# Transformer block on one core: shared keys for shared buffers in a build-time planner, and an earlier transpose of the first token block

## The chip, the cores and the metric

The kernel runs on one core of a Trainium2 chip. The metric is the device time of one execution in microseconds (us). All engines of the core work from their own instruction queues in order and wait for each other through semaphores: TensorE (PE in the profile; PEld is its weight load), VectorE (DVE), ScalarE (ACT), GpSimd (POOL) and SyncE (SP), which issues nearly all DMAs here.

## The reference

Input x is 8 x 1024 x 512 in float32, the condition 8 x 512. Hidden width is 2048, and there are 16 heads of 32.

```python
mod = silu(condition) @ Wada + bada
sh_a, sc_a, gt_a, sh_m, sc_m, gt_m = split(mod, 6, axis=1)
xm = layernorm(x, g1, be1) * (1 + sc_a) + sh_a
x = x + gt_a * (causal_attention(xm @ Wqkv) @ Wproj + bproj)
xm = layernorm(x, g2, be2) * (1 + sc_m) + sh_m
return x + gt_m * (gelu(xm @ W1 + b1) @ W2 + b2)
```

## The kernel before

**Tiling.** The tokens are cut into 16 blocks of 512 (two halves, h = 0 and 1, of each of 8 batch rows). A block passes through: normalisation into tiles `hat` (`normalize`), transposition and modulation into `xm` (`modulated`; its sums `t` for the fast products), K, Q and V, attention, the output projection (`project_out`), and the MLP (`up`, `down`). The weight products use Strassen's scheme (`strassen`, `down`): seven half-size products in place of eight, with sums of weight pieces and of activations, and partial results in tiles `p1`, `u2`, `u4`.

**Attention.** A head group is four heads. For each group, `scores` computes Q·K with one mask and one maximum over each strip (lines 1175, 1187, 1195); `split_maxima` splits the maxima into three bf16 parts `mcols` (lines 1216 to 1219), on GpSimd or VectorE; `maxima_rows` turns them into a row by matmul (line 1235). `weights_T` computes K·Q with the row subtracted (lines 1261 and 1272) and the exponential on ScalarE into one of three slots `pT` (line 1284), and GpSimd masks the diagonal (line 1289). `weigh` multiplies by V into `po` (line 1312). In `attend`, GpSimd adds each later strip into the first strip's `pT` (line 1396), in place: it may do so only when `weigh` has read that first strip. `finish` sums over partitions by matmul (line 1330); ScalarE copies that to `rec` and `po` to `top` (lines 1336 and 1339), VectorE inverts `rec` in four parts (line 1345), and GpSimd multiplies them into Q's place (line 1350). `rec`, `top`, `p1`, `u2` and `u4` have one buffer each, the tag `y` has two.

**PSUM.** The scores' tile `st` takes four banks, `po` one. The three others, `banks`, serve every linear product, the transposes, line 1235 and line 1330. `lin_bank` takes the one that is free soonest.

**Order.** The order of every engine's instructions is fixed while the program is built. A planner keeps a modelled clock for each engine (`now`) and two tables: `written[key]`, when a value is there, and `left[key]`, when its last reader is done.

```python
def due(reads=(), writes=()):
    t = 0.0
    for k in reads:
        t = max(t, written.get(k, 0.0))
    for k in writes:
        t = max(t, left.get(k, 0.0))
    return t
```

`sooner` and `either` pick the engine of a copy or sum from these, `split_maxima` picks its own, and `step_aside` decides before each attention step whether to issue linear work (the next matmuls of `plan`, four at a time) first. The linear work is a generator `linear` over `plan`, with side threads for transposes and the last products of a Strassen step; each yields what it will read and write, and `work` advances the one whose wait ends first. The hardware's own waits are by semaphores on the real buffers, so a wrong key makes the plan wrong but not the result. Where a key has the step's name in it (`("rec", n, g)`), the buffer's earlier user has another key, and the planner does not see that the write must wait for that user.

**Opening.** SyncE loads the condition, the first block, the eight pieces of Wada for `("mod", 0)` and `("mod", 1)`, and the pieces of K's weights. `modulation(i)` is 128 small matmuls (line 199 with 8 columns). `norm_columns` makes the gain and the shift on VectorE from both. Then `("at", 0)` starts the transposes of the first block (line 594) with their modulation on ScalarE or VectorE (lines 604 and 598), and `("k", 0)` issues its four weight sums on VectorE (line 649) and the first products (line 199).

Of the kernel before, what the change touches and what calls it, by code (L numbers as in the profile page):

```python
# [22 lines left out]
def kernel(  # L23
# [201 lines left out]
    def mlp_steps(n):  # L225
        return [("u", n, i) for i in range(NQ)] + [("d", n, part) for part in range(4)]

    plan = {
        -1: [("mod", 0), ("mod", 1), ("norm_columns_a",), ("at", 0), ("load_xa", 1)]
        + [("k", 0), ("norm_a", 1), ("q", 0), ("at", 1), ("v", 0)],  # L230
        0: [("load_xa", 2), ("preps",), ("k", 1), ("norm_a", 2), ("gates", "a"), ("q", 1)]
        + [("mod", 3), ("at", 2), ("v", 1), ("mod", 4), ("k", 2), ("gates", "m"), ("columns_m",)],
# [175 lines left out]
    def modulation(i):  # L408
        at = take(4)
        part = {kf: halves(j) for kf, j in zip(RAW, at)}  # L410
        yield [], [BANK]
        bank = lin_bank()
        pm = banks[bank][:, : NC * B].rearrange("p (c b) -> p c b", b=B)
        for c in range(NC):
            for k in range(NC):
                w = part[k // 2, c // 2][:, k % 2, ts(c % 2, P)]
                matmul(pm[:, c, :], w, condT[:, k, :], k == 0, k == NC - 1, bank=bank)
                note("PE", 90)
                yield [], []
        release(*at)  # L420
        combine_out(
            modT[:, ts(i, NC), :],
            bank,
            pm,
            cols[:, O_BADA + i * NC : O_BADA + (i + 1) * NC].unsqueeze(2).to_broadcast([P, NC, B]),
        )
# [16 lines left out]
        return gain, shift  # L443

    columns_of = {}
    gate_rows = {}

    kept_rows = {}
# [115 lines left out]
        for t in range(NTT):  # L564
            add_job(lambda t=t: statistics(t), [sources[t]], key[0] == "m")

    def modulated(key, gain, shift, b, guards):
        for t in ("B11", "B21", "B22", "T1", "T2", "T3", "T4"):
            written[key, t] = NEVER
        yield [("hat", key, 0), *guards], [BANK]  # L570
        got = hats.pop(key)
        xm = act.tile([P, NC, TB], F32, tag="xm", name=f"xm_{key}")
        sums = act.tile([P, 3, 2, HB], F32, tag="t", name=f"t_{key}")
        one, two = slice(0, 2), slice(2, 4)
        left_half, right_half = slice(0, HB), slice(HB, TB)
        part = {
            "B11": xm[:, one, left_half],
            "B21": xm[:, two, left_half],
            "B22": xm[:, two, right_half],
            "T1": xm[:, one, right_half],  # L580
            "T2": sums[:, 0, :, :],
            "T3": sums[:, 1, :, :],
            "T4": sums[:, 2, :, :],
        }
        xm_of[key] = part
        at = {t: (key, t) for t in part}
        for c in range(NC):
            if c:
                yield [("hat", key, 0)], [BANK]
            bank = lin_bank()  # L590
            for t in range(NTT):
                if t:
                    yield [("hat", key, t)], []
                nc.tensor.transpose(banks[bank][:, ts(t, P)], got[t][:, ts(c, P)], ident)  # L594
                note_pe(TR, "whole", [("hat", key, t)], [("l", bank)])
            writes = [at["B11"], at["T1"]] if c < 2 else [at["B21"], at["B22"]]
            if sooner([("l", bank)], writes, 770, 780) == "DVE":
                nc.vector.tensor_scalar(
                    xm[:, c, :], banks[bank], gain[:, c, b : b + 1], shift[:, c, b : b + 1],
                    ALU.mult, ALU.add,  # L600
                )
                note("DVE", 770, [("l", bank)], writes)
            else:
                nc.scalar.activation(
                    xm[:, c, :], banks[bank], AF.Identity,
                    bias=shift[:, c, b : b + 1], scale=gain[:, c, b : b + 1],
                )
                note_act(780, None, [("l", bank)], writes)
            live[bank] = False
            if c == 1:  # L610
                nc.vector.tensor_tensor(part["T1"], part["T1"], part["B11"], ALU.subtract)
                note("DVE", 700, [at["B11"], at["T1"]], [at["T1"]], port=True)
        nc.vector.tensor_tensor(part["T2"], part["B22"], part["T1"], ALU.subtract)  # L613
        note("DVE", 700, [at["B22"], at["T1"]], [at["T2"]], port=True)
        for out, a, b in (("T3", "T2", "B11"), ("T4", "B21", "T2")):
            either(part[out], part[a], part[b], ALU.subtract, [at[a], at[b]], [at[out]])
# [74 lines left out]
    def strassen(step, x, dest, target, row, done):  # L691
# [43 lines left out]
        def partial(kind):  # L735
            return tmp.tile([P, 2, HB], F32, tag=kind, name=f"{kind}_{name}", bufs=1)

        k1, k2, k4 = (("part", name, i) for i in (1, 2, 4))
        a = yield from product("A11", "B11")
        p1 = partial("p1")  # L740
        copy_out(p1, a, blocks_of(a), [k1], last=False)
# [66 lines left out]
        )  # L808

    residual, stored = {}, {}  # L810
    LANDING = 10000

    def add_to(xt, other, reads, writes, op=ALU.add):
# [2 lines left out]
    def project_out(n):  # L816
        at = take(NC)
        yield [("attended", n)], []
        attT = qTs.pop(n)
        tiles = [residual[n][:, t, :] for t in range(NTT)]  # L820
        for t, xt in enumerate(tiles):
            xt_job = lambda t=t, xt=xt: add_to(xt, gate_rows["gba"], [("row", "gba")], [("xr", n, t)])
            pool_jobs.append((xt_job, [("xr", n, t)]))
        for t, xt in enumerate(tiles):
            bank = yield from accumulate(
                [(attT[:, c, ts(t, P)], piece(at[c])) for c in range(NC)], [("att", n)]
            )
            tag, bufs = ("hat", NTT) if n == NB - 1 else ("y", 2)
            y = tmp.tile([P, D], F32, tag=tag, name=f"y_{n}_{t}", bufs=bufs)
            ky = ("y", n, t)  # L830
            combine_out(y, bank, banks[bank], gate_rows["ga"], [("row", "ga")], [ky], ALU.mult)
            add_to(xt, y, [ky], [("xr", n, t)])
        release(*at)
        run_pool_jobs(True)
        normalize(tiles, f"m{n}", [("xr", n, t) for t in range(NTT)])
# [50 lines left out]
    def down(n, part):  # L886
# [42 lines left out]
            return tmp.tile([P, 2, HB], F32, tag=tag, name=f"{kind}_d_{n}", bufs=bufs)  # L929

        def key(kind):
            return ("down", n, kind)

        got = partials
        if part == 0:
# [10 lines left out]
        elif part == 1:  # L946
            bank, ps = yield from product("B22")
            got["v3"] = stage("v3", "y", 2)
            combine_out(got["v3"], bank, ps, got["u5"], [key("u5")], [key("v3")])
            combine(nc.vector, "B22", "B22", "B12")  # L950
            combine(nc.gpsimd, "B11", "B22", "B11")
            bank, ps = yield from product("B21")
            y = stage("y11", "y", 2)
            combine_out(y, bank, ps, got["u1"], [key("u1")], [key("y11")])
            combine(nc.gpsimd, "B21", "B21", "B22")
            settle(n, 0, 0, y, key("y11"))
# [7 lines left out]
        else:  # L964
# [6 lines left out]
            store(n, 1)  # L971
            bank, ps = yield from product("B21")
            y = stage("y21", "y", 2)
            combine_out(y, bank, ps, u3, [key("u3")], [key("y21")])
            settle(n, 1, 0, y, key("y21"))
            store(n, 0)
# [4 lines left out]
    def perform(step):  # L981
# [2 lines left out]
            yield from modulation(step[1])  # L984
        elif kind == "norm_columns_a":
            columns_of["a"] = norm_columns("a", 0, 1, O_G1, O_BE1)
        elif kind == "gates":
            yield from gates(step[1])
        elif kind == "columns_m":
# [20 lines left out]
        elif kind == "at":  # L1010
            n = step[1]
            guards = [("m used", n - 3)] if n > 2 else [("v done", 0)] if n == 2 else []
            start(modulated(f"a{n}", *columns_of["a"], blocks[n][0], guards))
        elif kind == "mt":
            n = step[1]
            guards = [("v done", n + 1)]
            start(modulated(f"m{n}", *columns_of["m"], blocks[n][0], guards))
        elif kind == "k":
            yield [("free for k", step[1])], []
            yield from project_T(step, kTs, kvp, "kT", lambda: None)  # L1020
# [33 lines left out]
    def start(it):  # L1054
        thread = [it, None]
        sides.append(thread)
        advance(thread)
# [264 lines left out]
    def finish(n, g):  # L1322
# [9 lines left out]
        free_p.append(slot)  # L1332
        top = tmp.tile([P, TB], F32, tag="top", name=f"top_{n}_{g}", bufs=1)
        rec = tmp.tile([P, TB], F32, tag="rec", name=f"rec_{n}_{g}", bufs=1)
        kr = ("rec", n, g)
        nc.scalar.copy(rec, banks[bank])  # L1336
        note_act(585, None, [("l", bank)], [kr])
        live[bank] = False
        nc.scalar.copy(top, outs.pop((n, g)))
        note_act(585, None, ["po"], [("top", n, g)])  # L1340
        part = TB // 4

        def invert(i):
# [4 lines left out]
        def quotient():  # L1348
            invert(3)
            nc.gpsimd.tensor_tensor(qTs[n][:, g, :], top, rec, ALU.mult)  # L1350
            note("POOL", 1285, [kr, ("top", n, g)], [("att", n)])
            if g == NC - 1:
                written["attended", n] = 0.0

# [4 lines left out]
    def attend():  # L1359
        previous = None  # L1360
        for n in range(NB):
# [19 lines left out]
            for g, k, upto in slots:  # L1381
# [9 lines left out]
                if k > 0:  # L1391
                    acc, first = totals[n, g]
                    for _, c0, w in parts:
                        for j in range(HPG):
                            into = acc[:, j, TB - w :]
                            nc.gpsimd.tensor_tensor(into, into, pT[:, j, c0 : c0 + w], ALU.add)  # L1396
                            note("POOL", 230 + 2.07 * w, [("p", slot), ("p", first)], [("acc", n, g)])
                previous = (n, g, parts, pT, slot, k == n_slots - 1)
                while unit_at[0] < upto:
                    ns = score_need(*units[unit_at[0]])  # L1400
# [109 lines left out]
```

## Time and profile before

| | us |
|---|---|
| median of 3 runs | 3730.38 |
| lowest to highest | 3725.5 to 3731.06 |
| profiled execution, own time | 3731.66 |
| its span in the trace | 3729.9 |
| TensorE busy in it | 3598.8 |
| VectorE busy | 2135.3 |
| GpSimd busy | 2034.5 |
| ScalarE busy | 1341.6 |

The mean granted TensorE clock of the profiled execution is 0.988. The trace repeats itself with every second token block, that is with every batch row, about every 452 us: the same instructions stand at 913.47, 1365.55 and 1817.72 us.

A timeline row has the start and the length in us, the engine, the line, the operation, the tile written and those read, shapes, the count of merged instructions, and in brackets the idle time of the engine before it with what ended it. A row of waits has the waiting instruction, what it waited for, the total in us, the number of times and the longest.

### The profile page before, as it was taken

What the parts mean: (1) busy time and instruction counts of PE and PEld (TensorE: products, weight loads), DVE (VectorE), ACT (ScalarE), POOL (GpSimd) and SP (SyncE); (2) the same over time, 40 slices, a digit from 0 to 9 for tenths busy, and PEclk for the clock granted to TensorE, in tenths of its full rate; (3) what the DMA queues carried; (4) which work ended last, traced back from release to release, by engine and by line L of the source; (5) the groups of instructions that cost most, each with busy time, mean ns of one, the idle gap of its engine ahead of it and who ended that gap; (6) DMA issues with size and microseconds to landing.
All of it is one profiled execution on the core that took longest, in us unless ns stands there. A gap on an engine that the chain in (4) does not pass through costs nothing.

```text
span 3729.9 us, 121143 instructions
## 1 busy us (share of the span) xinstructions
PE 3598.8 (96%) x54821; PEld 1769.8 (47%) x54821; DVE 2135.3 (57%) x2402; ACT 1341.6 (36%) x1436; POOL 2034.5 (55%) x2080
## 2 busy tenths in 40 slices
PE   8889999999999999999999999999999999998999
PEld 4424445444454444544445454444544445454445
DVE  5756665564745547465565665646556464654542
ACT  2334334252333524335152451524425243341421
POOL 1576645655455663566536664456654556444661
PEclk9989999999999999999999999999999999999999
DMA  6633333433334333433334333343333433234334
GB/s 200 196 117 99 116 92 105 127 104 117 106 110 119 105 121 106 138 97 98 120 106 135 97 98 117 106 133 103 101 112 106 135 103 118 91 106 123 90 108 132
DMA packets 307893, 430.34 MB, mean 115 GB/s; under 512 B 25900, under 2 KB 176236, under 8 KB 307380
## 3 DMA queue, kind: packets, MB, share of 16 engines
q1 hardware_dynamic: 307264, 422.56, 37.2%
q8 instruction: 432, 7.08, 0.8%
q14 instruction: 81, 0.66, 0.1%
q10 hardware_dynamic: 116, 0.03, 0.0%
HBM read 394.12 MB, written 28.38 MB: 113 GB/s over the span
## 4 chain that ended last, share of the span: by engine, by line
PE 85%; DVE 7%; POOL 3%; ACT 3%; issue 2%; DMA 0%; SPq 0%; ACTq 0%; POOLq 0%; DVEq 0%
PE bank L199 57%; PE st L1261 8%; PE sc L1175 8%; PE po L1312 7%; POOL pT L1396 2%; DVE mx L1195 2%; PE st L1272 2%; PE bank L594 2%; PE bank L1330 1%; DVE hT L901 1%; ACT pT L1284 1%; DVE xr L156 1%; ACT L546 1%; DVE sc L1187 1%; DVE rec L1345 1%
## 5 line engine op out<-in xcount | busy, mean ns | idle before, releaser
L1396 POOL TENSOR_TENSOR pT<-pT,pT 128x512 f32<-128x512 f32 (+3 forms) x1280 | 1201.9, 973 | 557.0 <-ACT pT L1284 386.0
L1284 ACT ACTIVATE pT<-st 128x2048 f32<-128x2048 f32 (+1 forms) x320 | 546.3, 1707 | 1061.9 <-PE st L1272 1007.4
L199 PE MATMUL bank<-w,hT 128*32 128x256 f32 x14336 | 810.0, 380 | 5.0 <-DVE hT L901 2.1
L1195 DVE TENSOR_REDUCE mx<-sc 128x4 f32<-128x2048 f32 (+3 forms) x384 | 668.9, 1756 | 216.2 <-PE sc L1175 209.0
L199 PEld LDWEIGHTS bank<-w,hT 128*32 128x32 f32 x14336 | 454.0, 110 | 358.4 <-issue 61.7
L199 PE MATMUL bank<-xm_m,w 128*32 128x256 f32 x8192 | 503.8, 380 | 0.5 <-DVE u_u L191 0.5
L1289 POOL TENSOR_SCALAR_AFFINE_SELECT pT<-pT 128x512 f32<-128x512 f32 x256 | 176.1, 700 | 553.1 <-ACT pT L1284 552.7
L199 PE MATMUL bank<-t_m,w 128*32 128x256 f32 x6144 | 384.4, 380 | 2.4 <-DVE t_m L613 1.0
L1261 PE MATMUL st<-qT,kT 32*128 32x512 f32 (+3 forms) x3072 | 343.1, 531 | 27.3 <-DVE mx L1195 27.2
L199 PEld LDWEIGHTS bank<-xm_m,w 128*32 128x32 f32 x8192 | 255.0, 110 | 238.7 <-issue 77.8
L1175 PE MATMUL sc<-kT,qT 32*128 32x512 f32 (+3 forms) x3072 | 344.7, 533 | 11.2 <-DVE mx L1195 6.6
L1187 DVE TENSOR_TENSOR sc<-sc,mask 128x512 f32<-128x512 f32 (+1 forms) x192 | 167.9, 875 | 320.6 <-PE sc L1175 286.5
L1312 PE MATMUL po<-pT,v 128*32 128x512 f32 (+3 forms) x3072 | 319.0, 503 | 4.5 <-POOL pT L1289 4.4
L199 PEld LDWEIGHTS bank<-t_m,w 128*32 128x32 f32 x6144 | 192.0, 110 | 179.6 <-issue 52.0
L199 PE MATMUL bank<-xm_a,w 128*32 128x256 f32 x3968 | 245.6, 383 | 10.0 <-ACT qT L186 4.9
L199 PE MATMUL bank<-w,qT 128*32 128x512 f32 x2048 | 249.3, 614 | 6.1 <-POOL qT L1350 3.2
L1345 DVE RECIPROCAL rec<-rec 128x128 f32<-128x128 f32 x256 | 224.0, 917 | 20.1 <-ACT rec L1336 20.1
L1261 PEld LDWEIGHTS st<-qT,kT 32*128 32x128 f32 x3072 | 128.1, 185 | 195.2 <-issue 67.8
L1175 PEld LDWEIGHTS sc<-kT,qT 32*128 32x128 f32 x3072 | 128.3, 186 | 185.6 <-ACT pT L1284 87.8
L191 DVE TENSOR_TENSOR hT<-bank,u_u 128x512 f32<-128x512 f32 x192 | 130.6, 686 | 122.4 <-PE bank L199 119.8
L199 PE MATMUL bank<-t_a,w 128*32 128x256 f32 x2944 | 186.4, 382 | 13.1 <-ACT rec L1336 13.1
L199 PEld LDWEIGHTS bank<-xm_a,w 128*32 128x32 f32 x3968 | 122.5, 110 | 120.5 <-issue 31.5
(181 smaller groups left out, 3536.9 us busy)
## 6 DMA issues: line engine op xcount, KB each, us to landing
w<-in_L_cond_W_dram SPq DMA_DIRECT2D x384, 256.0 KB, 2.9
w<-kept_up_S SPq DMA_DIRECT2D x256, 256.0 KB, 2.7
w<-kept_down_S SPq DMA_DIRECT2D x256, 256.0 KB, 2.6
w<-kept_qkv_S SPq DMA_DIRECT2D x180, 256.0 KB, 3.0
w<-in_L_cond_Wqkv_dram SPq DMA_DIRECT2D x147, 256.0 KB, 3.4
hat<-in_x_dram SPq DMA_DIRECT2D x64, 256.0 KB, 3.3
w<-in_L_cond_Wproj_dram SPq DMA_DIRECT2D x64, 256.0 KB, 3.2
xr<-in_x_dram SPq DMA_DIRECT2D x64, 256.0 KB, 4.6
```

The source lines that it names most:

```text
L191: nc.vector.tensor_tensor(out, src, other, op)
L199: nc.tensor.matmul(ps[r, :], lhsT[:, r], rhs, start=start, stop=stop, skip_group_check=True)
L594: nc.tensor.transpose(banks[bank][:, ts(t, P)], got[t][:, ts(c, P)], ident)
L1175: nc.tensor.matmul(sc[:, j, c0 : c0 + w], qTs[n][r, g, ts(qt, P)], keys_of(n, kh)[r, g, :w], start=True, stop=True, skip_group_check=True,)
L1187: nc.vector.tensor_tensor(diagonal, diagonal, mask[:, :span].unsqueeze(1).to_broadcast([P, HPG, span]), ALU.add,)
L1195: nc.vector.tensor_reduce(mx[:, kh, qt, :], sc[:, :, c0 : c0 + w], axis=AX.X, op=ALU.max)
L1261: nc.tensor.matmul(st[:, j, c0 : c0 + w], kT[r, g, ts(k % NTT, P)], qT[r, g, TB - w :], start=(c0 == 0), stop=False, skip_group_check=True,)
L1284: nc.scalar.activation(pT[:, :, :used], st[:, :, :used], AF.Exp, scale=scale)
L1289: nc.gpsimd.affine_select(diagonal, diagonal, pattern=[[0, HPG], [1, P]], compare_op=ALU.is_ge, fill=0.0, base=0, channel_multiplier=-1,)
L1312: nc.tensor.matmul(po[r, TB - w :], v[:, k % NTT, g * P + j * hd : g * P + (j + 1) * hd], pT[:, j, c0 : c0 + w], start=(k == 0), stop=last ...
L1345: nc.vector.reciprocal(some, some)
L1396: nc.gpsimd.tensor_tensor(into, into, pT[:, j, c0 : c0 + w], ALU.add)
```

## The change

It has two parts. In the first, keys of the planner's tables are named after the buffer instead of the step: `rec`, `top`, `p1`, `u2`, `u4`, and the two buffers of `y` in turn; and the accumulation of line 1396 counts the first strip's slot as written instead of read, so that the planner makes it wait for `weigh`. In the second, the first block's 16 transposes go into the scores' four banks and are issued between `("mod", 0)` and `("mod", 1)`, whose matmuls wait for the key `early` that is set when the transposes are issued; the modulation of its four chunks is issued after `norm_columns`. No arithmetic is added or taken away.

```diff
     plan = {
-        -1: [("mod", 0), ("mod", 1), ("norm_columns_a",), ("at", 0), ("load_xa", 1)]
+        -1: [("at", 0), ("mod", 0), ("mod", 1), ("norm_columns_a",), ("load_xa", 1)]
...
     def modulation(i):
...
-        yield [], [BANK]
+        yield ["early"] if i == 1 else [], [BANK]
...
+    written["columns"] = written["early"] = NEVER
...
-    def modulated(key, gain, shift, b, guards):
+    def modulated(key, b, guards):
...
+        def modulate(c, place, source):
+            gain, shift = columns_of[key[0]]
             writes = [at["B11"], at["T1"]] if c < 2 else [at["B21"], at["B22"]]
-            if sooner([("l", bank)], writes, 770, 780) == "DVE":
+            if sooner([source], writes, 770, 780) == "DVE":
...
+        if key == "a0":
+
+            early = ps_st.tile([P, NC, TB], F32, tag="st", name="early")
+        for c in range(NC):
+            if key != "a0":
+                if c:
+                    yield [("hat", key, 0)], [BANK]
+                bank = lin_bank()
+                place, source = banks[bank], ("l", bank)
+            else:
+                place, source = early[:, c, :], "st"
+            for t in range(NTT):
+                if t or c:
+                    yield [("hat", key, t)], []
+                nc.tensor.transpose(place[:, ts(t, P)], got[t][:, ts(c, P)], ident)
+                note_pe(TR, "whole", [("hat", key, t)], [source])
+            if key != "a0":
+                modulate(c, place, source)
+                live[bank] = False
+        if key == "a0":
+            written["early"] = 0.0
+            yield ["columns"], []
+            for c in range(NC):
+                modulate(c, early[:, c, :], "st")
...
-        k1, k2, k4 = (("part", name, i) for i in (1, 2, 4))
+        k1, k2, k4 = "p1", "u2", "u4"
...
+    y_count, y_keys = [0], {}
+
+    def y_key(kind, new=False):
+
+        if kind not in y_keys or new:
+            y_keys[kind] = ("y", y_count[0] % 2)
+            y_count[0] += 1
+        return y_keys[kind]
...
-            ky = ("y", n, t)
+            ky = ("y", n, t) if n == NB - 1 else y_key("proj", True)
...
         def key(kind):
-            return ("down", n, kind)
+            return {"u1": "p1", "u3": "p1", "u5": "u4", "u2": "u2"}.get(kind) or y_key(kind)
...
         elif kind == "norm_columns_a":
             columns_of["a"] = norm_columns("a", 0, 1, O_G1, O_BE1)
+            written["columns"] = 0.0
...
-        kr = ("rec", n, g)
+        kr = "rec"
...
-        note_act(585, None, ["po"], [("top", n, g)])
+        note_act(585, None, ["po"], ["top"])
...
-                            note("POOL", 230 + 2.07 * w, [("p", slot), ("p", first)], [("acc", n, g)])
+                            note("POOL", 230 + 2.07 * w, [("p", slot)], [("acc", n, g), ("p", first)])
```

More of the change, by code (lines that the diff above doesn't have):

```diff
@@ L586, in modulated @@
         at = {t: (key, t) for t in part}
[L587 to L595, printed above, removed]
+        def modulate(c, place, source):
+            gain, shift = columns_of[key[0]]
             writes = [at["B11"], at["T1"]] if c < 2 else [at["B21"], at["B22"]]
-            if sooner([("l", bank)], writes, 770, 780) == "DVE":
+            if sooner([source], writes, 770, 780) == "DVE":
                 nc.vector.tensor_scalar(
-                    xm[:, c, :], banks[bank], gain[:, c, b : b + 1], shift[:, c, b : b + 1],
+                    xm[:, c, :], place, gain[:, c, b : b + 1], shift[:, c, b : b + 1],
                     ALU.mult, ALU.add,
                 )
-                note("DVE", 770, [("l", bank)], writes)
+                note("DVE", 770, [source], writes)
             else:
                 nc.scalar.activation(
-                    xm[:, c, :], banks[bank], AF.Identity,
+                    xm[:, c, :], place, AF.Identity,
                     bias=shift[:, c, b : b + 1], scale=gain[:, c, b : b + 1],
                 )
-                note_act(780, None, [("l", bank)], writes)
-            live[bank] = False
+                note_act(780, None, [source], writes)
             if c == 1:
@@ L948, in down @@
             got["v3"] = stage("v3", "y", 2)
+            y_key("v3", True)
             combine_out(got["v3"], bank, ps, got["u5"], [key("u5")], [key("v3")])
@@ L953, in down @@
             y = stage("y11", "y", 2)
+            y_key("y11", True)
             combine_out(y, bank, ps, got["u1"], [key("u1")], [key("y11")])
@@ L973, in down @@
             y = stage("y21", "y", 2)
+            y_key("y21", True)
             combine_out(y, bank, ps, u3, [key("u3")], [key("y21")])
@@ L1012, in perform @@
             guards = [("m used", n - 3)] if n > 2 else [("v done", 0)] if n == 2 else []
-            start(modulated(f"a{n}", *columns_of["a"], blocks[n][0], guards))
+            start(modulated(f"a{n}", blocks[n][0], guards))
         elif kind == "mt":
@@ L1016, in perform @@
             guards = [("v done", n + 1)]
-            start(modulated(f"m{n}", *columns_of["m"], blocks[n][0], guards))
+            start(modulated(f"m{n}", blocks[n][0], guards))
         elif kind == "k":
@@ L1350, in quotient @@
             nc.gpsimd.tensor_tensor(qTs[n][:, g, :], top, rec, ALU.mult)
-            note("POOL", 1285, [kr, ("top", n, g)], [("att", n)])
+            note("POOL", 1285, [kr, "top"], [("att", n)])
             if g == NC - 1:
```

## The prediction

> **What bounds the kernel now.** I read the page first. TensorE is busy nearly all the time and its clock is full outside the opening and the end, so only its idle time and its slow stretches can be won back: 3729.9 - 3598.8 = 131 us, plus what a halved clock costs.
>
> ```profile
> PE 3598.8 (96%) x54821; PEld 1769.8 (47%) x54821; DVE 2135.3 (57%) x2402; ACT 1341.6 (36%) x1436; POOL 2034.5 (55%) x2080
> PEclk9989999999999999999999999999999999999999
> ```
>
> Next I read TensorE's own waits. The list is short, and two rows of it bear on keys that the change renames; the waits of the other engines show the buffer behind each.
>
> ```profile
> PE bank L1235 <- POOL mcols L1219: 19.8, 8, 2.8
> PE bank L199 <- ACT rec L1336: 13.6, 8, 1.9
> ...
> POOL pT L1396 <- PE po L1312: 163.4, 13, 20.9
> ...
> ACT rec L1336 <- POOL qT L1350: 37.3, 7, 5.3
> ```
>
> GpSimd's accumulation waits for the reader of its in-place target (L1312), and ScalarE's copy into the one buffer `rec` waits for the quotient that still reads it (L1350). Neither wait is in the planner's tables now. The timeline shows what they do to TensorE, once in every pair of blocks.
>
> ```profile
> 913.47 5.52 POOL L1396 TENSOR_TENSOR pT<-pT,pT 128x384 f32<-128x384 f32 x8 [11.25 <-PE po L1312]
> 918.93 0.25 POOL L1216 CAST mcols<-mx 128x16 bf16<-128x16 f32 x1
> 920.21 0.41 PE L1235 MATMUL bank<-ident_b,mcols 128*32 128x128 bf16 x16 [2.70 <-POOL mcols L1219]
> ...
> 961.65 1.26 POOL L1350 TENSOR_TENSOR qT<-top,rec 128x512 f32<-128x512 f32 x1 [3.33 <-DVE rec L1345]
> 962.94 0.58 ACT L1336 COPY rec<-bank 128x512 f32<-128x512 f32 x1 [5.33 <-POOL qT L1350]
> 963.58 1.93 PE L199 MATMUL bank<-t_a,w 128*32 128x256 f32 x32 [1.87 <-ACT rec L1336]
> ```
>
> Stall one: the maxima are ready at 916.07 (L1195, 914.85 + 1.22), but the split was given to GpSimd, which is in the accumulation until 919.0; TensorE stands still for 2.70 us. Stall two: a bank is held until `rec` may be written; TensorE stands still for 1.87 us, then 0.62 and 0.70 us more behind copies (p_q at 965.52, then qT) that stand behind `rec` on ScalarE.
>
> **Part by part: the accumulation's target counted.** Stall one comes seven times: 2.76 + 2.70 + 5 x 2.69 = 18.9 us. The clock follows it. The windows after six of the seven show the granted clock at half, the fourth does not:
>
> ```profile
> 921.50:924.80 3.30, 3.30 (x16) 0.52 (x8) 0.00 (x0) 0.00 (x0) 3.22 (x5) 0.50 0.00 0
> 1825.00:1828.40 3.40, 3.40 (x40) 1.06 (x36) 0.62 (x1) 0.50 (x1) 3.32 (x6) 1.00 0.00 0
> ```
>
> The Trainium skill (TensorE: Matmul & The Clock Gate, section "What's actually happening") has the clock halved only after an idle window of about 3.4 us; by it a gap of 2.7 us costs no clock, and the sum for this stall would be 18.9 us. The trace differs, so I price it from the trace: from the end of stall one to the end of stall two are the same instructions in every pair, and they take
>
> ```profile
> 1824.46 0.35 PE L1235 MATMUL bank<-ident_b,mcols 128*32 128x128 bf16 x12 [2.69 <-POOL mcols L1219]
> 1866.19 0.64 PE L199 MATMUL bank<-t_a,w 128*32 128x256 f32 x8 [1.88 <-ACT rec L1336]
> 2278.78 0.41 PE L1235 MATMUL bank<-ident_b,mcols 128*32 128x128 bf16 x16 [2.69 <-POOL mcols L1219]
> 2322.16 0.62 PE L199 MATMUL bank<-t_a,w 128*32 128x256 f32 x5 [1.88 <-ACT rec L1336]
> ```
>
> 41.73 us without a halved window, 43.38 with one, and in the last pair 44.59 with two (3185.28 to 3229.87): 1.65 for one, 2.86 for two. Five single ones and a double make 5 x 1.65 + 2.86 = 11.1 us. Together stall one is worth 30.0 us. That is the measured upper end; its lower end is that only the engine changes. The change lets the planner see GpSimd busy until 919, so it gives the split to VectorE. There, beside a running accumulation, the nearest row (944.05 to 946.79, another split beside L1396) takes 0.20 + 0.51 + 0.96 + 0.96 = 2.63 us against four pitches of 0.33 on GpSimd. Starting behind the y combine at 916.73 it ends at 919.4, and L1235 starts some 0.7 us earlier than 920.21: 7 x 0.7 = 5 us. But the planner will also see, for the first time, that the split takes until then, and `step_aside` then issues linear matmuls in the gap. They are there: the projection's matmuls (w,qT) go on right behind the stall, in an accumulation that already has its bank. At the nearest row, 944.92, 64 such matmuls stood in the gap and L1235 waited for nothing. I take 26 of the 30, leaving half a microsecond at each place for a fill that comes in whole groups of four.
>
> **rec and top counted.** Stall two is 1.88 + 0.62 + 0.70 = 3.2 us, seven times: 22.4 us at most. The planner will now know that the bank is held, but I see nothing it could run instead. The tile `st` waits for the maxima that VectorE ends at 965.07, the K tail's banks wait for combines behind VectorE's four reciprocals (958.21, 3.35 us), and `rec` cannot be written before 962.9 whatever is planned. What it can do is put p_q and qT on VectorE, off the queue behind `rec`, `top` and the table load; VectorE is free for them at 965.07, against 965.52 on ScalarE. I take 0.6 us each, 4 us. Bounds: 22.4 us gained; 5 us lost (0.7 each) if the copies then queue behind a reduction.
>
> **p1, u2, u4, y counted.** No row of TensorE's waits names such a reuse with more than a single case (y, 2.8 us at 3395.65, in the last block, whose keys stay). I take nothing; bounds 5 us either way. A change of order at these places is covered by the linear work that keeps TensorE at 98% to 100% between the stalls.
>
> **The opening.** The transposes leave the place behind the second modulation and stand in front of it:
>
> ```profile
> 13.00 2.93 ACT L557 ACTIVATE hat<-hat,offset_a,rstd_a 128x512 f32<-128x512 f32 x4 [0.44 <-DVE offset_a L549]
> 17.56 0.72 PE L199 MATMUL bank<-condT,w 128*32 128x8 f32 x40 [2.74 <-issue]
> 18.21 3.68 PE L594 MATMUL bank<-ident,hat 128*128 128x128 f32 x16
> 19.40 0.78 ACT L604 ACTIVATE xm_a<-bank,shifta,gaina 128x512 f32<-128x512 f32 x1 [3.47 <-PE bank L594]
> 22.62 3.64 PE L199 MATMUL bank<-xm_a,w 128*32 128x256 f32 x32 [0.73 <-DVE xm_a L598]
> ```
>
> They need the fourth `hat`, at 15.93. Thirteen remain then, at a pitch of 0.226 us ((3.68 - 0.29) / 15) and a tail of 0.29: 19.1. Behind them in TensorE's queue stand all 128 matmuls of the second modulation, 2.25 us by their rows (64 in 1.17 to 1.22, so 0.016 us each, plus a tail): 21.35. VectorE takes the modulation off at 18.35 now, and gain and shift are there 1.05 us later, at 19.40: so 22.4. The last chunk that the first product waits for is now on VectorE, behind the four weight sums (21.76, 0.80 us). After the change the chunks go one after another on ScalarE, since VectorE is in those sums: the second ends at 24.05, and the first product starts at 24.1 instead of 22.62. Loss 1.5 us. The gain side: the idle 2.74 us ahead of 17.56, which no semaphore ends, would lie under the wait for `hat`; if the clock, full from about 27.1, keeps its place in time, half the loss comes back. The loss side: if that idle time belongs to the instructions and comes again behind the transposes, 1.5 + 2.7 = 4.2 us. Bounds +4.2 and -1; I take +1.5. SyncE's queue issues the four `hat` loads of the second block and five weight loads after these steps, some 3 us later; they are needed at 34 us and later, so that is hidden.
>
> **The sum**, against the profiled execution: 3731.7 - 26 - 4 + 1.5 = 3703.2. It stood 1.3 above the median of the runs, so 3702.
>
> **The rivals.** *Nothing to run in the gaps.* The engine moves, the gap stays: -5 + 0 + 1.5, about 3727. For: stall two is such a place. Against: the projection's matmuls stand right behind stall one.
>
> *Bank shortage, slower.* The linear matmuls pulled forward end their accumulation earlier, and its bank then waits for a VectorE that is in a 2.63 us split; with three banks, the next linear product or the row of L1235 finds none. The price is that of stall two, 3.2 us (4.85 with a halved window). Once per pair it nearly cancels the gain: 7 x 3.2 = 22. Once per block it gives 15 x 3.2 = 48 - 28.5 = +19.5, so 3750. It decides from nine such waits on (28.5 / 3.2). For: stall two shows that three banks do run out, and one changed choice repeats in every pair. Against: VectorE is idle for 8.45 us behind stall one.
>
> *Both stalls go.* The order around `rec` shifts enough that its quotient is early: -30 - 22.4 + 1.5, about 3681. For: the new `rec` time moves every later choice. Against: the reciprocals' place is set by VectorE's load, which does not shrink.
>
> That the change doesn't reach the places at all is excluded by the rows: the two buffers waited for are the two whose keys change.
>
> **How the numbers follow.** A difference under 0.2% (7.5 us) is about what a measurement of this kernel can't tell from none. Likeliest case 0.55, with its own range 3684 to 3722, from the 30 and 22 us above and 10 us for the opening and the end, where TensorE already waits for VectorE; both stalls gone 0.11; nothing to run 0.12, within 0.2%; bank shortage 0.22. Faster 0.66, same 0.12, slower 0.22. The range, 3678 to 3744, leaves out the far ends of the last and of the case of both stalls.
>
> **What would show it.** Right: L1235's wait for L1219 under 5 us in all; fewer than 29 splits on GpSimd; no halved windows near 921, 1372, 2280; stall two's row still there; the first large product at about 24. Wrong: a new row of TensorE's waits with seven or more cases, for a bank held by DVE or ACT; or half-clock windows at new places in each pair.

## The result, and the profile after

The changed kernel takes 3686.66 us (median of 4 runs, 3685.5 to 3686.95) against 3729.83 for the kernel before in the same comparison: a ratio of 0.9886, 95% interval 0.9869 to 0.9903. The profiled execution took 3685.5 us, with a span of 3683.6 and a mean granted clock of 0.992.

The page of the changed kernel, first the busy times, then the granted clock in forty slices:

```profile
PE 3578.0 (97%) x54821; PEld 1770.6 (48%) x54821; DVE 2158.7 (59%) x2455; ACT 1330.8 (36%) x1415; POOL 2030.0 (55%) x2052
PEclk9989999999999999999999999999999999999999
```

TensorE issues the same 54821 matmuls and is busy 20.8 us less: the halved windows that are gone are part of that. Its idle time fell by 25.5 us, from 131.1 to 105.6. The forty slices are too coarse to show halved windows of 3 us, which is why the clock has to be looked up in stretches. VectorE became busier, by 23.4 us.

TensorE's waits in the changed kernel (lines of attention now stand 31 further down: L1266 was L1235, L1250 was L1219, L1367 was L1336, L1292 was L1261):

```profile
PE st L1292 <- DVE mx L1226: 34.7, 38, 4.6
...
PE bank L199 <- DVE sums_k L668: 2.6, 1, 2.6
...
PE bank L1266 <- POOL mcols L1250: 0.9, 1, 0.9
...
PE bank L199 <- ACT rec L1367: 0.5, 1, 0.5
```

Both stalls are gone: 19.8 us in 8 waits became 0.9 in one, and 13.6 in 8 became 0.5 in one. Two things are new. One wait of 2.6 us for the weight sums `sums_k` is from the opening. The wait of `st` for the maxima grew from 27.2 us (24 times) to 34.7 (38 times); among the new ones are seven of 0.87 us behind the transposes of L622, one in each pair from 510 us on, and seven of 0.20 us some 10 us later. The longer one, in the pair that the next two excerpts show:

```profile
957.14 1.15 PE L1292 MATMUL st<-qT,kT 32*128 32x384 f32 x16 [0.87 <-DVE mx L1226]
```

The place of stall one, in the timeline of the changed kernel (start, length, engine, line, operation, tiles; idle time before in brackets):

```profile
910.80 5.55 POOL L1427 TENSOR_TENSOR pT<-pT,pT 128x384 f32<-128x384 f32 x8 [11.25 <-PE po L1343]
...
912.18 1.22 DVE L1226 TENSOR_REDUCE mx<-sc 128x4 f32<-128x1024 f32 x1
...
913.44 0.35 DVE L1247 CAST mcols<-mx 128x16 bf16<-128x16 f32 x1
...
914.77 1.92 PE L199 MATMUL bank<-w,qT 128*32 128x512 f32 x16
...
915.19 0.41 DVE L1250 TENSOR_TENSOR mcols<-rest,mcols 128x16 bf16<-128x16 f32 x1
915.48 0.68 DVE L191 TENSOR_TENSOR y<-bank,row_ga 128x512 f32<-128x512 f32 x1
...
916.51 0.41 PE L1266 MATMUL bank<-ident_b,mcols 128*32 128x128 bf16 x16
```

GpSimd is still in the accumulation, until 916.35. The split is on VectorE and done at 915.6, and 16 matmuls of the projection stand on TensorE in the gap. L1266 follows them without a wait. The granted clock is full from 910 to 925.

The place of stall two:

```profile
931.99 0.69 DVE L539 BATCH_NORM_STATS2 st_m<-xr 128x6 f32<-128x512 f32 x1
...
942.21 0.68 DVE L539 BATCH_NORM_STATS2 st_m<-xr 128x6 f32<-128x512 f32 x1
...
948.25 3.38 DVE L1376 RECIPROCAL rec<-rec 128x128 f32<-128x128 f32 x4
```

The reciprocals start 37.45 us after the accumulation's start, where they started 44.7 us after it before (958.21 less 913.47). The quotient is over early enough that ScalarE's copy into `rec` stands at 954.57 without holding a bank. Why they are early is the question that the experiments answer.

Each profiled execution can be cut at the second and at the fourteenth block's load of `xr`, which are six pairs of blocks apart:

| us | start to the 2nd load | six pairs | rest | clock at half, 300 to 3300 us |
|---|---|---|---|---|
| before | 454.6 | 2718.4 | 557.0 | 23.9 |
| after | 458.9 | 2679.0 | 545.6 | 0 |
| difference | +4.3 | -39.4 | -11.4 | |

The six pairs give back 6.57 us each. By the prediction's prices, stall one is 2.69 us, its halved window 1.65 in five of these six pairs, and stall two 3.2; less the new 0.87 and 0.20 that is 6.2 on average. So the prices were about right, and the question is why both stalls went.

### The profile page after: what moved, and what is told of

It is laid out like the page before. It is cut to its first block, busy times and chain, and to the rows that moved or that the text cites. A ratio compares the mean times of both kernels' runs of the same rounds, so it can differ in the third digit from the quotient of the medians.

```text
span 3683.6 us, 121126 instructions
## 1 busy us (share of the span) xinstructions
PE 3578.0 (97%) x54821; PEld 1770.6 (48%) x54821; DVE 2158.7 (59%) x2455; ACT 1330.8 (36%) x1415; POOL 2030.0 (55%) x2052
## 4 chain that ended last, share of the span: by engine, by line
PE 86%; DVE 7%; ACT 2%; POOL 2%; issue 2%; DMA 0%; SPq 0%; ACTq 0%; POOLq 0%; DVEq 0%
PE bank L199 58%; PE st L1292 8%; PE sc L1206 8%; PE po L1343 7%; DVE mx L1226 2%; PE st L1303 2%; PE bank L1361 2%; POOL pT L1427 1%; PE bank L622 1%; ACT pT L1315 1%; DVE hT L928 1%; DVE sc L1218 1%; DVE xr L156 1%; DVE t_m L156 1%; PE bank L1266 0%
## 5 line engine op out<-in xcount | busy, mean ns | idle before, releaser
L1292 PE MATMUL st<-qT,kT 32*128 32x512 f32 (+3 forms) x3072 | 342.9, 530 | 35.9 <-DVE mx L1226 34.7
L199 PE MATMUL bank<-w,qT 128*32 128x512 f32 x2048 | 241.5, 598 | 6.1 <-POOL qT L1381 3.2
L1292 PEld LDWEIGHTS st<-qT,kT 32*128 32x128 f32 x3072 | 129.7, 185 | 201.9 <-issue 60.6
```

The lines of the kernel that those rows point to most:

```text
L199: nc.tensor.matmul(ps[r, :], lhsT[:, r], rhs, start=start, stop=stop, skip_group_check=True)
L1292: nc.tensor.matmul(st[:, j, c0 : c0 + w], kT[r, g, ts(k % NTT, P)], qT[r, g, TB - w :], start=(c0 == 0), stop=False, skip_group_check=True,)
```

## The experiments

**The four parts alone.** Each kernel is the one before with one part of the change. The first counts only the accumulation's target:

```diff
-  note("POOL", 230 + 2.07 * w, [("p", slot), ("p", first)], [("acc", n, g)])
+  note("POOL", 230 + 2.07 * w, [("p", slot)], [("acc", n, g), ("p", first)])
```

> The kernel before with one edit: the accumulation of line 1396 counts the first strip's slot as written. Theory A (each key removes its own stall): stall one and the halved windows behind it go, 30 us, and stall two stays (seven rows of about 1.9 us of TensorE behind the copy into rec); 3700 us. Rival B (stall two goes because the order behind stall one is a new one, whatever key rec has): both stalls go; about 3680 us. Rival C (only the engine of the split changes, the gap stays): 3725 us.

3682.17 us against 3725.99 (ratio 0.9885, interval 0.987 to 0.9899): the whole gain, and stall two went with stall one, though the keys of `rec` and `top` are still the old ones. The waits of this kernel, with the old line numbers:

```profile
PE bank L1235 <- POOL mcols L1219: 1.4, 2, 0.9
...
PE bank L199 <- ACT rec L1336: 0.5, 1, 0.5
```

The second counts only `rec` and `top`:

```diff
-  kr = ("rec", n, g)
+  kr = "rec"
-  note_act(585, None, ["po"], [("top", n, g)])
+  note_act(585, None, ["po"], ["top"])
```

> The kernel before with only the keys of rec and top shared. Theory A (each key removes its own stall): stall two goes, up to 22 us, stall one stays with its halved windows; 3708 us. Rival B (rec's key does little, the prediction's view): only the copies behind rec move, 4 us; 3726 us, and the seven waits of TensorE for the copy into rec remain.

3718.76 us, ratio 0.9983 (0.9973 to 0.9992): about 6 us. Its waits:

```profile
PE bank L1235 <- POOL mcols L1219: 19.9, 8, 2.8
PE bank L199 <- ACT rec L1336: 13.1, 7, 1.9
```

Both stalls stand as before. What went is the 0.62 and 0.70 us behind the copies p_q and qT, which no longer have rows. So the key that names the buffer of stall two doesn't remove stall two. How the two short waits went is seen behind one stall two of this kernel:

```profile
962.02 1.15 PE L1261 MATMUL st<-qT,kT 32*128 32x384 f32 x16
962.11 0.57 ACT L186 COPY p_q<-bank 128x512 f32<-128x512 f32 x1
...
966.18 0.69 DVE L183 COPY qT<-bank 128x512 f32<-128x512 f32 x1 [0.47 <-PE bank L199]
```

The copy qT moved to VectorE, here and at the six other places. The copy p_q stays on ScalarE in all 16 blocks; TensorE now runs attention matmuls (962.02 and on) while it waits for that bank.

The third has only `p1`, `u2`, `u4` and `y` named after their buffers:

```diff
-  k1, k2, k4 = (("part", name, i) for i in (1, 2, 4))
+  k1, k2, k4 = "p1", "u2", "u4"
-  ky = ("y", n, t)
+  ky = ("y", n, t) if n == NB - 1 else y_key("proj", True)
...
```

> The kernel before with only the keys of p1, u2, u4 and y shared. Theory A: no row of TensorE's waits named their reuse, so nothing, 3730 us within 5. Rival B (a part of the gain beyond stall one is theirs, through the choice between VectorE and ScalarE for copies): 3710 to 3722 us.

3724.36 us, ratio 0.9999 (0.999 to 1.0009): nothing.

The fourth is the changed kernel with all keys put back, so that only the opening differs from before (`p1`, `u2`, `u4` and `y` likewise):

```diff
-  kr = "rec"
+  kr = ("rec", n, g)
-  note("POOL", 230 + 2.07 * w, [("p", slot)], [("acc", n, g), ("p", first)])
+  note("POOL", 230 + 2.07 * w, [("p", slot), ("p", first)], [("acc", n, g)])
...
```

> The changed kernel with the keys of the planner put back: only the first block's transposes are ahead of the second modulation. Theory A: the first large product starts at 22.7 us as before, but the four weight sums now stand behind the activations' sums on VectorE, so the second product waits 2.6 us for them and the clock is halved until 33.9 us; slower by 4 to 6 us, 3735 us. Rival B (the loss is swallowed by the waits for VectorE's maxima between 175 and 275 us): 3730 us.

3730.29 us, ratio 1.0009 (0.9999 to 1.0019): 4 us more than the kernel before, which this comparison does not tell from none.

**What removes stall one: the engine or the fill?** Two kernels separate them. In the first, the kernel before gets a second clock for GpSimd that counts the accumulation's wait and is used for the choice of the split's engine alone. Seven splits move to VectorE; TensorE's order is the old one, instruction by instruction.

```diff
+  aware[0] = max(aware[0], due(reads, [*writes, *more])) + ns    # in note, for POOL
...
-  on_pool = max(now["POOL"], ready) + 1000 < max(now["DVE"], ready) + 2200
+  on_pool = max(aware[0], ready) + 1000 < max(now["DVE"], ready) + 2200
...
-  note("POOL", 230 + 2.07 * w, [("p", slot), ("p", first)], [("acc", n, g)])
+  note("POOL", 230 + 2.07 * w, [("p", slot), ("p", first)], [("acc", n, g)], more=[("p", first)])
```

> The kernel before, in which only split_maxima picks its engine with the accumulation's wait counted: seven splits go from GpSimd to VectorE, TensorE's order stays as it was. Theory A (the gain comes from the linear matmuls that the planner puts into the gap, the engine does little): the split stands behind the y combine on VectorE and ends about half a us earlier, stall one is 2 us in place of 2.7, some halved windows stay, stall two stays; 3722 us. Rival B (the engine alone does it): stall one gone; 3698 us.

3704.42 us against 3725.87, ratio 0.9938 (0.9923 to 0.9952): 21.5 us from the engine alone. The timeline of this kernel at stall one (lines 3 further down than before):

```profile
907.51 1.22 DVE L1198 TENSOR_REDUCE mx<-sc 128x4 f32<-128x1024 f32 x1
...
908.77 0.35 DVE L1219 CAST mcols<-mx 128x16 bf16<-128x16 f32 x1
...
910.51 0.41 DVE L1222 TENSOR_TENSOR mcols<-rest,mcols 128x16 bf16<-128x16 f32 x1
910.80 0.68 DVE L194 TENSOR_TENSOR y<-bank,row_ga 128x512 f32<-128x512 f32 x1
...
910.98 0.41 PE L1238 MATMUL bank<-ident_b,mcols 128*32 128x128 bf16 x16 [0.80 <-DVE mcols L1222]
```

The split starts right behind the reduction, ahead of the y combine, and takes 2.15 us. The gap is 0.80 us instead of 2.70, and the clock is never at half between 300 and 3300 us. By the prediction's prices that is 18.9 - 5.7 + 11.1 = 24.3 us, near the 21.5 measured. Its waits still hold stall two:

```profile
PE bank L202 <- ACT rec L1339: 13.6, 8, 1.9
...
PE bank L1238 <- DVE mcols L1222: 5.7, 7, 0.9
```

The second kernel does the opposite: all keys of the change, the old opening, and the choice of the engine made by a clock of GpSimd that does not count the accumulation's wait. The seven splits stay on GpSimd, and the planner knows how late they are.

```diff
+  unaware[0] = max(unaware[0], due(reads, writes if seen is None else seen)) + ns    # in note, for POOL
...
-  on_pool = max(now["POOL"], ready) + 1000 < max(now["DVE"], ready) + 2200
+  on_pool = max(unaware[0], ready) + 1000 < max(now["DVE"], ready) + 2200
...
-  note("POOL", 230 + 2.07 * w, [("p", slot)], [("acc", n, g), ("p", first)])
+  note("POOL", 230 + 2.07 * w, [("p", slot)], [("acc", n, g), ("p", first)], seen=[("acc", n, g)])
```

> All the new keys, the opening as before, but split_maxima picks its engine without the accumulation's wait, so the seven splits stay on GpSimd, and the planner knows when they end. Theory A (the fill is what counts): linear matmuls stand in the gap although the split ends as late as before; no stall one, no halved windows, stall two gone too; 3682 to 3686 us. Rival B (it needs the engine): stall one stays; 3715 us.

3670.36 us (3669.48 to 3673.63), ratio 0.985 (0.9833 to 0.9866): faster than the change itself. The timeline of this kernel at the same place:

```profile
904.92 6.01 POOL L1410 TENSOR_TENSOR pT<-pT,pT 128x384 f32<-128x384 f32 x8 [11.24 <-PE po L1326]
...
908.90 3.64 PE L202 MATMUL bank<-w,qT 128*32 128x512 f32 x32
...
910.87 0.26 POOL L1230 CAST mcols<-mx 128x16 bf16<-128x16 f32 x1
...
912.35 0.41 PE L1249 MATMUL bank<-ident_b,mcols 128*32 128x128 bf16 x16
```

The split is as late as before, behind an accumulation of 6 us, and costs nothing: 32 matmuls fill the gap instead of 16. So either part removes stall one alone, the engine nearly and the fill wholly; where the fill is there, moving the engine is a loss: the same keys with the splits on VectorE take 3682.71 us (below).

**What removes stall two?** In the kernel before, VectorE's rows ahead of the reciprocals at stall two are these:

```profile
955.01 0.68 DVE L538 BATCH_NORM_STATS2 st_m<-xr 128x6 f32<-128x512 f32 x1
...
957.42 0.66 DVE L538 BATCH_NORM_STATS2 st_m<-xr 128x6 f32<-128x512 f32 x1
...
958.21 3.35 DVE L1345 RECIPROCAL rec<-rec 128x128 f32<-128x128 f32 x4
```

Four statistics of the second normalisation stand there, 3.2 us in all: they are queued ahead of other waiting jobs. The experiment takes that priority away, its only edit of the kernel before:

```diff
-  add_job(lambda t=t: statistics(t), [sources[t]], key[0] == "m")
+  add_job(lambda t=t: statistics(t), [sources[t]])
```

> The kernel before with one edit: the MLP's normalisation statistics are no longer put ahead of the waiting reciprocals in VectorE's list of jobs. Theory A (stall two exists because four statistics, 3.2 us, stand ahead of the four reciprocals, so that the quotient and the copy into rec are late; with the accumulation counted the residual rows are done earlier and the statistics fall before that place): stall two goes without the accumulation or rec touched, 22 us; 3704 to 3710 us. Rival B (stall two hangs on something else, such as VectorE's whole load): stays within 5 us of 3726.

3704.94 us, ratio 0.9943 (0.9928 to 0.9958): 21 us. Its timeline, with the reciprocals and the statistics in the other order:

```profile
950.56 3.38 DVE L1345 RECIPROCAL rec<-rec 128x128 f32<-128x128 f32 x4
...
953.85 0.64 DVE L538 BATCH_NORM_STATS2 st_m<-xr 128x6 f32<-128x512 f32 x1
954.02 1.28 POOL L1350 TENSOR_TENSOR qT<-top,rec 128x512 f32<-128x512 f32 x1
...
955.33 0.59 ACT L1336 COPY rec<-bank 128x512 f32<-128x512 f32 x1 [2.17 <-POOL qT L1350]
```

And its waits: stall one stands, stall two is gone.

```profile
PE bank L1235 <- POOL mcols L1219: 20.5, 9, 2.8
...
PE bank L199 <- ACT rec L1336: 0.5, 1, 0.5
```

TensorE's order is the old one until behind the first place of stall two (510 us), where that stall is already gone; from 512 us on the planner orders some matmuls differently too. So stall two was the order of two jobs on VectorE, and the wait for `rec` only the place where it came out. In the changed kernel the same priority is still there, but the statistics come before they can be in the way: three of them at 931.99 to 934.5, the fourth at 942.21. What they wait for is earlier, because the projection's matmuls were pulled forward into stall one: VectorE's addition of `row_gba` into the residual rows is at 931.39, 20.6 us after the accumulation's start, where it was at 938.45, 25.0 us after it. Of the 7.3 us by which the reciprocals came earlier, 3.2 are the statistics; the rest is about stall one with its halved window (4.3), whose loss alone leaves stall two, as the kernel with the engine alone shows. That the keys of `rec` have no part in it is shown by the first experiment; that the fill is the link is supported, though not isolated, by the kernel with the engine alone, where TensorE's order is the old one and stall two stays.

**The opening.** The timeline of the changed kernel:

```profile
16.02 3.04 PE L622 MATMUL early<-ident,hat 128*128 128x128 f32 x13 [0.23 <-ACT hat L558]
...
18.99 1.69 PE L199 MATMUL bank<-condT,w 128*32 128x8 f32 x128
...
22.66 3.26 PE L199 MATMUL bank<-xm_a,w 128*32 128x256 f32 x32 [1.98 <-ACT xm_a L599]
...
25.98 1.75 DVE L668 TENSOR_TENSOR sums_k<-w,w 128x512 f32<-128x512 f32 x1
...
28.52 3.64 PE L199 MATMUL bank<-t_a,sums_k 128*32 128x256 f32 x32 [2.60 <-DVE sums_k L668]
...
34.60 1.90 PE L199 MATMUL bank<-xm_a,sums_k 128*32 128x256 f32 x32
```

The last row, the fourth product, starts 11.9 us behind the first. In the kernel before it started 7.4 us behind it, at 30.04:

```profile
30.04 1.90 PE L199 MATMUL bank<-xm_a,sums_k 128*32 128x256 f32 x32
```

The transposes and the second modulation stand back to back, and the first product starts at 22.66, as before. But the second product waits 2.60 us for weight sums that VectorE now takes up at 25.98, behind the sums of activations. The clock stays at half from 23.6 to 33.85 us:

```profile
23.60:33.85 10.25, 7.65 (x76) 3.37 (x72) 6.04 (x8) 1.60 (x3) 1.76 (x1) 0.50 0.72 252
33.85:40.00 6.15, 6.15 (x120) 3.36 (x113) 2.35 (x4) 0.59 (x1) 0.00 (x0) 1.00 0.01 3
```

(Window, length, busy time and count of PE, PEld, DVE, ACT and POOL, granted clock, DMA share and GB/s.) The reason is in the code: `("k", 0)` now waits for the key `columns` before it issues anything, its weight sums included. An edit of the changed kernel sets that key behind the sums:

```diff
-  written["columns"] = 0.0     # in perform, behind norm_columns
...
   w = weight_sums(step, part)
+  written["columns"] = 0.0     # in strassen
```

> The changed kernel with one edit in the opening: the first block's modulation is let go only when the four weight sums of K have been issued on VectorE. Theory A (the opening's loss is the second product's wait of 2.6 us for those sums and the half clock that follows it): the wait goes, 3 to 5 us faster than the changed kernel; 3682 us. Rival B (the loss is in the transposes ahead of the modulation, or is swallowed later): within 1.5 us of 3686.7.

The fourth product then starts 7.0 us behind the first (29.35 less 22.31), so the slip is where the opening lost its time. With the opening alone changed, the distance is 11.0 us. The stretch up to the second `xr` load fell from 458.9 to 454.8 us, the same as before the change, but the whole is 3685.34 us, ratio 0.9888 (0.9873 to 0.9903): 1.3 us less than the change, not distinguishable from it. The part behind the fourteenth load is 2.3 us longer in this execution, 547.9 against 545.6. There the granted clock between 3300 and 3650 us is 0.97, against 0.99 in the changed kernel: three halved windows more, which at 1.65 us each is more than the difference.

**All keys, and the two best together.** The change without its opening, that is the diffs of the first three kernels above together:

> The changed kernel with the opening put back: all the new keys, nothing else. Theory A (the accumulation's target alone carries the gain, the other keys nothing beside it, and the opening costs 3 to 5 us): 3682 us, as with the accumulation alone. Rival B (the opening costs nothing here): 3686.7 us.

3682.71 us, ratio 0.9887 (0.987 to 0.9903), level with the first experiment's 3682.17: on top of the accumulation's key the other keys add nothing. It is 4 us under the change, but the two were compared with different runs of the kernel before (3725.5 and 3729.83), and as ratios they are level (0.9887 and 0.9886).

The mended opening together with the splits left on GpSimd, that is the changed kernel with the diff that moves `columns` and the one that brings in `unaware`:

> All the new keys with the seven splits kept on GpSimd, and the transposes ahead of the second modulation with the four weight sums ahead of the first block's modulation. Theory A (the mended opening is level with the old one): 3670 us within 3, as with the old opening. Rival B (the earlier transposes bring something once nothing stands behind the sums): 3664 us.

3670.69 us, ratio 0.9852 (0.9837 to 0.9867): level with the 3670.36 of the same kernel with the old opening. So the earlier transposes, as they were made, delay the first products by 3.6 to 4.5 us, which the whole times do not resolve from none; with their slip mended they bring nothing that these runs can tell.

The version with all keys, the old opening and the seven splits on GpSimd is the best of them all, 3670.36 us. Against the same keys with the splits on VectorE, its six pairs take 2669.9 us instead of 2680.1. First the wait for the maxima in that best kernel, then in the one with all keys:

```profile
PE st L1275 <- DVE mx L1209: 26.7, 22, 4.5
```

```profile
PE st L1272 <- DVE mx L1206: 34.0, 36, 4.2
```

7.3 us of the 12 between the two kernels lie in this row; VectorE is 17 us less busy (2142.4 against 2159.2), so that it can end the maxima sooner. The kernel with all keys also has two halved windows in its six pairs that the other has not, 3.3 us at 1.65 each. The rest was not traced.

## Why the prediction was partly right

**Faster, by the accumulation's key: right.** The stall one price held: gone whole, with its halved windows. The fill that the prediction named is there, and the kernel with the splits left on GpSimd shows that it is enough alone. The 26 us of 30 were, if anything, cautious.

**The step "only the engine changes: 7 x 0.7 = 5 us": wrong.** It measured 21.5. The error was the place of the split in VectorE's queue: it was put behind the y combine, at 916.73, but it is issued right behind the reduction that makes its input. And 0.8 us of remaining gap no longer halved the clock, which the 5 us did not count. The rival *nothing to run in the gaps* at 3727 was therefore mispriced: without any fill the kernel is at 3704.

**The step "rec and top counted: 4 us": near for that edit, wrong for the sum.** The edit alone gives about 6 us and leaves the 1.88 us. Its way was half as described: qT went to VectorE, but p_q stayed on ScalarE, and there was something to run meanwhile: the matmuls into `st`, whose maxima are ready by then. But the sum holds 4 of the 22.4 us of stall two, and the term measured 22.4 less seven new waits of 0.87 and of 0.20, 14.9. This is most of where 3702 missed 3687: with all 30 us of stall one, 14.9 in place of 4 and 4.3 in place of 1.5, the same sum gives 3690. The failed argument is "the reciprocals' place is set by VectorE's load, which does not shrink". The load even grew, by 23.4 us, and the reciprocals came earlier all the same, because four statistics no longer stood ahead of them. What was read as load was order. The rival that both stalls go, at 3681 (3679.5 with the 1.3 us that the main sum takes off), given a chance of 0.11, is what happened; its reason (that the time of `rec` moves later choices) was wrong, as the kernel with only that key shows. That 3687 still lies in the range 3684 to 3722 of the likeliest case is luck: in that case stall two stays.

**p1, u2, u4 and y: right**, nothing: TensorE's order is the old one, instruction by instruction.

**The opening, +1.5 with bounds -1 and +4.2: the way was wrong, the size is open.** The stretch up to the second `xr` load is 4.3 us longer in the profile and the fourth product 4.5 us later behind the first, near the upper bound, but by another way than that bound's. In the seven other kernels with the old opening that stretch lies between 450.8 and 456.7 us, so a single execution does not fix the size. The prediction delayed the first product to 24.1, and it started at 22.66: the 128 small matmuls took 1.69 us, not 2.25, and the idle 2.74 us ahead of the modulation did not come again. The loss is one product later, in the weight sums that the prediction left ahead of the modulated chunks on VectorE, as they are issued in the kernel before.

**Bank shortage, the slower rival: not there.** No new row with a bank held by VectorE or ScalarE comes once per block or per pair; the only new waits that do are those of 0.87 and 0.20 us for the maxima.

**What would show it.** L1235's wait under 5 us, fewer splits on GpSimd (22 of 64) and no halved windows near 921, 1372 and 2280 came as written. Stall two's row still there and a first product at 24 did not.

## What to carry to other kernels

When a stall ends on a buffer, look one step further back, at what stands ahead of its releaser on that engine's queue: a job with priority there can be the whole cause, and then no key of the buffer removes the stall. A planner that knows about a wait was worth more here for the work it puts into the gap than for moving the late step to another engine; when one corrected time feeds both choices, try each alone. When a step is moved earlier, look also at what now waits for its new key and is issued later than before.

## What the runs showed of the hardware that was not expected

The halved clock does not follow a gap of given length in a fixed way. Stall one, 2.7 us long seven times, came with 23.9 us of half clock in the kernel before, 27.3 with only `rec` and `top` renamed, 10.2 with only the parts, and 20.5 with the reciprocals first. Where the gaps at these places were 0.8 us there was none. With only the parts renamed TensorE's order is that of the kernel before, so the order does not decide it.

The traces show what does. All changes of the granted clock in one trace lie on a grid of 3.413 us: in the kernel before, halved windows begin at 467.45, 921.43 and 1371.99, which is 133 and 132 steps apart. Where the grid stands differs from execution to execution. What counts is how much of a gap falls into one window of the grid. First a window around stall one in the kernel before, with the next window:

```profile
918.01:921.43 3.42, 1.22 (x36) 0.81 (x40) 0.00 (x0) 1.16 (x2) 3.19 (x9) 1.00 0.00 0
921.43:924.84 3.41, 3.41 (x20) 0.52 (x8) 0.00 (x0) 0.00 (x0) 3.33 (x5) 0.50 0.00 0
```

Then two neighbouring windows of the kernel with only the parts, with the same gap cut by the grid:

```profile
917.46:920.88 3.42, 2.06 (x27) 0.56 (x16) 1.28 (x2) 1.02 (x1) 3.42 (x6) 1.00 0.01 4
920.88:924.29 3.41, 2.06 (x41) 0.82 (x41) 0.00 (x0) 0.59 (x1) 3.10 (x8) 1.00 0.00 0
```

In the first, TensorE is idle for 2.20 of 3.42 us, and the next window is at half clock. In the others it is idle for 1.36 and 1.35 us, and no window is halved. In the twelve traces together, between 40 and 3650 us, a window at full clock was followed by a halved one in all 95 cases with 2.1 us of idle time or more, in none of 12286 with less than 1.65, and in 23 of 73 between; what decides there was not found. Short gaps in one window add up: with the accumulation's key alone, 0.72 and 0.94 us were followed by a halved window at 2379.96. The Trainium skill (TensorE: Matmul & The Clock Gate, section "What's actually happening") asks for an idle window of about 3.4 us; here 2.1 us of one were always enough. A gap of 2.7 us can fall on either side of an edge, so it is priced as a chance, from as many repeats as the trace has.

The spread of the kernel before goes with the granted clock: its 41 runs beside the experiments took 3727.9 to 3733.6 us at a clock of 0.987 or 0.988, and 3719.9 to 3724.8 at 0.991 or 0.992.

A split of 128x16 elements, four instructions on VectorE, took 2.15 us beside a running accumulation on GpSimd (908.77 to 910.92), and 2.74 us at another place in the kernel before (944.05 to 946.79). On GpSimd, behind the accumulation, the same four took 1.24 us (910.87 to 912.11).
